# An attention and mixture-of-experts kernel on one Trainium2 core: the last routed block's products in another order, and the Silu of every block issued between its two halves

## Chip, core and metric

The kernel runs on one core of a Trainium2 chip. The metric is device time in microseconds, the median of several runs; smaller is better. The engines are TensorE (PE: matrix products; its weight loads are listed apart as PEld), VectorE (DVE), ScalarE (ACT), GpSimd (POOL) and SyncE (SP), which here only issues DMAs. Each engine carries out its own instructions in the order in which the program issues them, and waits on semaphores for the others.

## What is computed

The input is x of 8 x 256 rows, 512 long. A first layer adds a gated long convolution of the normalised x; it takes the first half of the time and isn't touched. The second layer, of the normalised result, is a mixture of experts of 2048 tokens:

```python
shared_out = silu(xf @ shared_wg.T) * (xf @ shared_wu.T) @ shared_wd.T      # inner width 704
h = silu(einsum('td,efd->etf', xf, exp_wg)) * einsum('td,efd->etf', xf, exp_wu)   # 8 experts, inner width 352
all_out = einsum('etf,edf->etd', h, exp_wd)
out = x + shared_out + sum over the 2 chosen experts of topk_w * all_out
```

All of it is float32. Only the two chosen experts of a token are computed.

## The kernel before

**Blocks.** The tokens are sorted by expert on the chip into blocks of up to 128 rows. 33 blocks are always worked through (`NSURE`): 25 with one expert each, 4 whose two halves of 64 rows have an expert each, and 4 in four groups of 32 rows, the last three groups of one expert. 20 more half-blocks stand inside an `If` (`rest_of_blocks`, L1875), which this input skips. The loop of L1887 takes the blocks in the order `seq`; the last one (`last`, index 32) is a block of one expert.

**One block.** A block's rows are gathered from `xn_d` by an indirect DMA of POOL, stored and reloaded by SP's DMAs in turned squares, and transposed by DVE (`block_T`). Then:

- `block_up` (L1776): the up products into a PSUM tile `up` of two halves, `ps[:, 0]` (gate) and `ps[:, 1]` (up). A half is 512 float32 wide, of which 352 are used, and fills one bank. For a block of one expert these are 4 products per half, issued half 0 first, then half 1; the trace lists each product as two passes. After all of them ACT takes the Silu of half 0 (L1790), and DVE multiplies it by half 1 (L1793; in the last block L1800, in an order that suits a transpose on PE).
- `block_hT` (L1818) transposes the result on DVE in 16 pieces. The last block uses `last_hT` (L1808) instead: three transposes on PE (L1813), copied from PSUM by ACT (L1814) and DVE (L1815).
- `block_down` (L1833): three down products (L1841, six passes) into a PSUM tile `y`, the scaling by the gate on ACT (`ys`, L1850), and an indirect DMA of POOL that adds the rows to `out` (L1854). These scatter-adds are ordered among themselves, since two of them can name the same row.

In the loop the down product of a block is issued two blocks later (L1908), so that its transposes are done; in the last three rounds it is the block before (L1910). The round of the last but two issues two down products.

**The end.** The shared expert's down products of the last two token tiles (`LATE`) are left for the end. `late_products` (L1916) issues them: for each tile five products of 512 columns (two passes each), and one of the short remainder (L1938). PE's order there is: up products of the last block, down product of the last but one, three transposes, one late product, down product of the last block, and the other late products. When the last scatter-add has landed, SP and ACT reload the two tiles' rows of `out` (L1934), DVE adds the late products (L1947), and SP and ACT store them (L1948).

**Order and waits.** The program is scheduled by hand (`manual_schedule`, L110): every engine gets its instructions in the order of the source. The waits between engines are made from the tiles that each instruction reads and writes. The shared expert's products (`seven`, L831) also use a two-bank PSUM tile, whose banks are written by PE and copied by ACT (L856) by turns; there, the program declares each product of one bank and each copy of the other to be independent:

```python
def free_of(ins, others):
    for other in others:
        tc.declare_no_dep(ins.ins, other.ins, reason="it is of the other bank")
```

`block_up` makes no such declaration.

Of the kernel before, what the change touches and what calls it, by code (L numbers as in the profile page):

```python
# [22 lines left out]
NLB = L // P  # L23
# [4 lines left out]
FF = 352  # L28
F_TILES = [(0, 128), (128, 128), (256, 96)]
SFF = 2 * FF  # L30
NSF = 6
# [47 lines left out]
def tile_xattn_moe(  # L79
# [29 lines left out]
    V, G, A, T, S = nc.vector, nc.gpsimd, nc.scalar, nc.tensor, nc.sync  # L109
# [993 lines left out]
    for c in range(NCHUNK):  # L1103
# [6 lines left out]
        if c == NCHUNK - 2:  # L1110
            at = len(steps) - TPC
# [319 lines left out]
    for h in range(H):  # L1431
# [15 lines left out]
        c, r = divmod(h - 10, 8)  # L1447
        nine, picks_here = h >= H9, c >= 0 and r == 2
        ready = done < h - 10 and steps[done][0] <= h
        between = copies = None  # L1450
        if c >= 0 and r == 7:
            make_down_sums(c, 0)
        if ready and is_begun(*steps[done][1:]):

            def between(at=steps[done][1:]):
                begun[at] = (begin_seven if at[0] is up_step else begin_down)(*at[1:])
                for _ in begun[at][0]():
                    pass
# [151 lines left out]
    wgu_sb = wgu_pool.tile([P, NEXP, NGU], F32, name="wgu_sb")  # L1610

    def load_wgu(e, n=2):
        m = 2 * NLB
        A.dma_start(
            out=wgu_sb[:, e : e + n].rearrange("p e (c f) -> p (e c) f", f=FF),
            in_=egu[e * m : (e + n) * m].rearrange("c p f -> p c f"),
        )
# [42 lines left out]
    xgs, xTs, eks = {}, {}, {}  # L1660
# [11 lines left out]
    def rows_in(b):  # L1672
        return P if b < NSURE else HP
# [27 lines left out]
    def load_ek(b):  # L1701

        i = b - NPURE
        e = nc.values_load(
            ek[0:1, b : b + 1] if i < 0 else eh[0:1, i : i + 1], engines=[PE], min_val=0,
            max_val=NEXP - 1 if i >= 0 else min(b, NEXP - 1),
            skip_runtime_bounds_check_because="an expert is a count of at most seven",
        )
        n = (P if i < 0 else Q if NPAIR <= i < NMIX else HP)
        eks[b] = [(slice(0, n), e)]  # L1710
        if 0 <= i < NMIX:
            eks[b] += [(slice(at, at + n), OWN[i]) for at in range(n, P, n)]

    def weights(sb, b, e, at, n):
        most = NEXP if b >= NPURE else min(b + 1, NEXP)
        w = sb[:, :most].rearrange("p e f -> p (e f)")
        at = e * sb.shape[2] + at
        return w[:, at : at + n] if isinstance(e, int) else w[:, bass.ds(at, n)]

    def block_T(b):  # L1720

        own = (rows, 3) if b < NSURE else (spare, 1)
        nq = rows_in(b) // Q
        xTs[b] = own[0].tile([P, NLB, NQ, Q], F32, tag="xT", name=f"xT_{b}", bufs=own[1])
        V.transpose(  # L1725
            xTs[b][:, :, :nq].rearrange("p k c b -> p c k b"),
            xgs.pop(b)[:, :nq].rearrange("p c (k a) -> p c k a", a=Q),
        )
# [4 lines left out]
    seq = list(range(NPURE))  # L1733
# [21 lines left out]
    def load_wd(e):  # L1755
        if e >= NEXP:
            return
        wde = wd_sb[:, e].rearrange("p (t d) -> p t d", d=L)
        S.dma_start(
            out=wde[:, 0:2, :], in_=ed[e, 0 : 2 * P].rearrange("(t p) d -> p t d", p=P)  # L1760
        )
        S.dma_start(out=wde[: FF - 2 * P, 2, :], in_=ed[e, 2 * P : FF])
# [10 lines left out]
    NF = len(F_TILES)  # L1773
    hs, hTb = {}, {}

    def block_up(k, last):  # L1776
        n = rows_in(k)
        ps = (ps_b if k < NSURE else ps_spare).tile([P, 2, L], F32, tag="up", name=f"up_{k}")
        for m in range(2):
            for j in range(NLB):  # L1780
                for at, e in eks[k]:
                    T.matmul(  # L1782
                        ps[at, m, :FF],
                        lhsT=xTs[k][:, j].rearrange("p c b -> p (c b)")[:, at],
                        rhs=weights(wgu_sb, k, e, (m * NLB + j) * FF, FF),
                        start=(j == 0),
                        stop=(j == NLB - 1),
                    )
        hk = (blk if k < NSURE else spare).tile([P, FF], F32, tag="h", name=f"h_{k}")
        A.activation(hk[:n], ps[:n, 0, :FF], AF.Silu)  # L1790
        xTs.pop(k)
        if not last:
            V.tensor_tensor(hk[:n], hk[:n], ps[:n, 1, :FF], ALU.mult)  # L1793
            hs[k] = hk
            return

        hp = blk.tile([P, NF, NQ, Q], F32, tag="h", name=f"hp_{k}")
        for q0, q1, n in ((0, NQ - 1, NF), (NQ - 1, NQ, NF - 1)):
            squares = slice(q0 * NF * Q, (q0 * NF + (q1 - q0) * n) * Q)
            V.tensor_tensor(  # L1800
                hp[:, :n, q0:q1].rearrange("p t q a -> p q t a"),
                hk[:, squares].rearrange("p (q t a) -> p q t a", t=n, a=Q),
                ps[:, 1, squares].rearrange("p (q t a) -> p q t a", t=n, a=Q),
                ALU.mult,
            )
        hs[k] = hp

    def last_hT(k):  # L1808
        hp = hs.pop(k).rearrange("p t q a -> p (t q a)")
        pt = ps_y.tile([P, NF, P], F32, tag="dn", name=f"hT_ps_{k}")  # L1810
        hT = blk.tile([P, NF, NQ, Q], F32, tag="hT", name=f"hTb_{k}")
        for ft, (f0, fw) in enumerate(F_TILES):
            T.transpose(pt[:fw, ft], hp[:, f0 : f0 + fw], ident)  # L1813
        A.copy(hT[:, : NF - 1].rearrange("p t c b -> p t (c b)"), pt[:, : NF - 1])  # L1814
        V.tensor_copy(hT[:fw, NF - 1].rearrange("p c b -> p (c b)"), pt[:fw, NF - 1])  # L1815
        hTb[k] = hT
# [16 lines left out]
    def block_down(k):  # L1833
        if k < NSURE:
            ps = ps_y.tile([P, L], F32, tag="dn", name=f"y_{k}")
        else:
            ps = ps_spare.tile([P, 2, L], F32, tag="up", name=f"y_{k}")[:, 0]
        hT = hTb.pop(k)
        for ft, (_, fw) in enumerate(F_TILES):
            for at, e in eks[k]:  # L1840
                T.matmul(  # L1841
                    ps[at],
                    lhsT=hT[:fw, ft].rearrange("p c b -> p (c b)")[:, at],
                    rhs=weights(wd_sb, k, e, ft * L, L)[:fw],
                    start=(ft == 0),
                    stop=(ft == NF - 1),
                )
        y = (blk if k < NSURE else spare).tile([P, L], F32, tag="y", name=f"ys_{k}", bufs=4 if k < NSURE else 1)
        n = rows_in(k)
        A.activation(y[:n], ps[:n], AF.Copy, scale=gate[:n, k : k + 1])  # L1850


        def send(at, index, col):
            G.indirect_dma_start(  # L1854
                out=out,
                out_offset=bass.IndirectOffsetOnAxis(
                    ap=index[: at.stop - at.start, col : col + 1], axis=0
                ),
                in_=y[at],
                in_offset=None,  # L1860
                bounds_check=NTOK + P - 1,
                oob_is_err=True,
                compute_op=ALU.add,
            )

        send(eks[k][0][0], row, k)
        if len(eks[k]) > 1:
            late.append((send, slice(eks[k][0][0].stop, P), second_row, k - NPURE))
# [17 lines left out]
    last = NSURE - 1  # L1886
    for k in range(NSURE):  # L1887
        if k + AHEAD < NSURE:
            load_ek(seq[k + AHEAD])
            if k > 0:  # L1890
                block_T(seq[k + AHEAD])
        if k > 0:
            load_wd(k + 1)
        if k in (2, 4):
            load_wgu(NEXP - 3 + k // 2, 1)
        if k + AHEAD + 3 < NSURE:
            gather(seq[k + AHEAD + 3])

        if k + AHEAD + 2 < NSURE:
            bring(seq[k + AHEAD + 2])  # L1900
        send_late()
        if k == REST_AT:
            rest_of_blocks()
        block_up(seq[k], k == last)
        if k < last:
            block_hT(seq[k])

        if 2 <= k < last - 1:  # L1908
            block_down(seq[k - 2])
        if k >= last - 2:  # L1910
            block_down(seq[k - 1])

    ps = ps_b.tile([P, LATE, L], F32, tag="up", name="dn_late")
    cols = [slice((TPC - LATE + i) * P, (TPC - LATE + i + 1) * P) for i in range(LATE)]

    def late_products(i, fts):  # L1916
        for ft in fts:
            T.matmul(
                ps[:, i],
                lhsT=hTs[last_c][:, ft, cols[i]],  # L1920
                rhs=wshd[:, ft, :],
                start=(ft == 0),
                stop=False,
            )

    last_hT(seq[last])
    late_products(0, range(1))
    block_down(seq[last])
    late_products(0, range(1, NSF - 1))
    late_rows = []  # L1930
    for i in range(LATE):
        t = NT - LATE + i
# [3 lines left out]
    for i in range(LATE):  # L1936
        at = slice(i * LAST, (i + 1) * LAST)
        T.matmul(  # L1938
            ps[:, i],
            lhsT=hTs[last_c][at, NSF - 1, cols[i]],  # L1940
            rhs=wshd[at, NSF - 1, :],
            start=False,
            stop=True,
# [98 lines left out]
```

## Time and profile before

| what | value |
|---|---|
| median of 3 runs | 738.3 us (738.06 to 738.66) |
| profiled execution, own time | 734.04 us |
| its span, first to last instruction | 732.2 us |
| mean granted TensorE clock | 0.999 |
| routed blocks, first up product to the last scatter's issue | 470.07 to 719.62 us |
| executed Silus of L1790 | 33 |
| DMA, mean over the span | 180 GB/s |

The profile is of a single execution, taken by the hardware profiler. A row of a timeline gives the start in us from the first instruction, the length, the engine, the source line and operation, the tiles (out<-in) and the number of merged instructions; in brackets stands how long the engine was idle before it and which instruction ended that. A row of the groups gives busy us and the mean ns of one instruction, then the idle us before the group and what ended it. The releaser is inferred from semaphores. Ends of matmuls are modelled, so successive passes overlap on paper; the time from start to start is what a pass costs in a stream.

### The profile page before, as it was taken

What the parts mean: (1) busy time and instruction counts of PE and PEld (TensorE: products, weight loads), DVE (VectorE), ACT (ScalarE), POOL (GpSimd) and SP (SyncE); (2) the same over time, 40 slices, a digit from 0 to 9 for tenths busy, and PEclk for the clock granted to TensorE, in tenths of its full rate; (3) what the DMA queues carried; (4) which work ended last, traced back from release to release, by engine and by line L of the source; (5) the groups of instructions that cost most, each with busy time, mean ns of one, the idle gap of its engine ahead of it and who ended that gap; (6) DMA issues with size and microseconds to landing.
All of it is one profiled execution on the core that took longest, in us unless ns stands there. A gap on an engine that the chain in (4) does not pass through costs nothing. (4 is left out here: it accounts for less than half of the span.)

```text
span 732.2 us, 10457 instructions
## 1 busy us (share of the span) xinstructions
PE 721.0 (98%) x3189; PEld 386.2 (53%) x3189; DVE 533.3 (73%) x1209; ACT 227.3 (31%) x459; POOL 405.4 (55%) x433
## 2 busy tenths in 40 slices
PE   9999999999999999999999999999999999999996
PEld 4333336555455655555665478455445444555552
DVE  4788889878677987777987574386786767758740
ACT  2222245745316554426435132011111111111110
POOL 7899898489776388794380422113344534424221
PEclk9999999999999999999999999999999999999999
DMA  8657748556635466525354968599876676666533
GB/s 284 226 186 276 282 141 267 181 121 193 205 106 193 136 163 195 178 86 170 112 130 139 378 180 276 178 278 313 242 170 127 124 157 149 128 156 146 88 43 86
DMA packets 91276, 131.62 MB, mean 180 GB/s; under 512 B 10896, under 2 KB 54928, under 8 KB 91216
## 3 DMA queue, kind: packets, MB, share of 16 engines
q1 hardware_dynamic: 69648, 93.37, 40.7%
q0 software_dynamic: 8544, 17.34, 13.2%
q10 hardware_dynamic: 13024, 20.19, 7.9%
q8 instruction: 28, 0.46, 0.2%
q14 instruction: 32, 0.26, 0.1%
HBM read 93.86 MB, written 37.00 MB: 179 GB/s over the span
## 5 line engine op out<-in xcount | busy, mean ns | idle before, releaser
L509 PE MATMUL cv<-kv,tz 64*64 64x512 f32 (+1 forms) x976 | 184.4, 597 | 0.3 <-DVE prod L585 0.3
L1782 PE MATMUL up<-wgu_sb,xT 128*128 (+5 forms) x784 | 162.4, 461 | 0.4 <-PEq L1876 0.4
L1825 DVE STREAM_TRANSPOSE hTb<-h 32x96 f32<-32x96 f32 (+1 forms) x512 | 133.8, 261 | 7.8
L460 POOL TENSOR_TENSOR kv<-vT,ctxT 128x512 f32<-128x512 f32 x127 | 131.6, 1069 | 11.9 <-DVE top L743 3.9
L1782 PEld LDWEIGHTS up<-wgu_sb,xT 128*128 128x128 f32 (+2 forms) x784 | 92.2, 155 | 75.3 <-issue 33.4
L509 PEld LDWEIGHTS cv<-kv,tz 64*64 64x64 f32 (+1 forms) x976 | 65.1, 145 | 109.5 <-issue 87.4
L1854 POOL DMA_INDIRECT out_dram<-ys,row x33 | 50.5, 1529 | 123.5 <-DMA out_dram<-ys,row 38.7
L1841 PE MATMUL y<-wd_sb,hTb 128*128 (+11 forms) x294 | 91.0, 595 | 0.0
L585 DVE TENSOR_TENSOR prod<-cv,ctxT 128x1024 f32<-128x1024 f32 x64 | 78.2, 1221 | 15.8 <-PE cv L509 14.1
L594 DVE TENSOR_REDUCE convT<-prod 128x128 f32<-128x1024 f32 x64 | 78.1, 1220 | 2.2
L844 PE MATMUL gu<-tb,wst 128*128 128x256 f32 x320 | 78.6, 381 | 0.6 <-ACT g L856 0.4
L1680 POOL DMA_INDIRECT picked<-xn_d,row x33 | 35.0, 1061 | 64.9 <-PE halves_ps L1317 19.5
L844 PEld LDWEIGHTS gu<-tb,wst 128*128 128x128 f32 x320 | 60.3, 190 | 17.3 <-issue 7.9
L1790 ACT ACTIVATE h<-up 128x352 f32<-128x352 f32 x33 | 15.3, 463 | 145.4 <-PE up L1782 145.4
L844 PE MATMUL gu<-xfT,wst 128*128 128x256 f32 x240 | 60.1, 386 | 0.2 <-DVE prod L585 0.2
L640 POOL TENSOR_TENSOR skip<-ctxT,w 128x512 f32<-128x512 f32 x16 | 17.2, 1075 | 74.6 <-DVE cv L582 38.7
L1841 PEld LDWEIGHTS y<-wd_sb,hTb 128*128 128x128 f32 (+5 forms) x294 | 34.3, 155 | 44.0 <-issue 38.7
L844 PEld LDWEIGHTS gu<-xfT,wst 128*128 128x128 f32 x240 | 44.2, 190 | 18.6 <-issue 12.1
L1850 ACT ACTIVATE ys<-y,gate 128x512 f32<-128x512 f32 x33 | 22.7, 687 | 73.1 <-PE y L1841 68.0
L509 PE MATMUL cv<-kv,td 128*128 128x512 f32 x88 | 45.2, 596 | 0.0
L801 POOL DMA_INDIRECT table<-entries,to x32 | 31.5, 985 | 19.2 <-DVE at L797 10.7
L1725 DVE STREAM_TRANSPOSE xT<-xg 128x512 f32<-128x512 f32 x33 | 23.5, 711 | 24.7 <-DMA xg<-picked_d 22.0
(266 smaller groups left out, 820.5 us busy)
## 6 DMA issues: line engine op xcount, KB each, us to landing
wst<-wst_d SPq DMA_DIRECT2D x17, 896.0 KB
tz<-in_toep_dram SPq DMA_DIRECT2D x32, 384.0 KB
wgu_sb<-in_egu_dram ACTq DMA_DIRECT2D x3, 2816.0 KB
picked_d<-picked SPq DMA_DIRECT2D x33, 256.0 KB
xg<-picked_d SPq DMA_DIRECT2D x132, 64.0 KB
ctxT<-in_cT_dram SPq DMA_DIRECT2D x16, 384.0 KB
x<-in_xv_dram SPq DMA_DIRECT2D x16, 256.0 KB
x<-in_x_dram SPq DMA_DIRECT2D x16, 256.0 KB
```

The lines of the kernel that those rows point to most:

```text
L460: engine.tensor_tensor(kvs[h][:, at], v[:, :, cols].unsqueeze(2).to_broadcast([P, B, NH, NH]), ctxT[t][:, at, :, cols].unsqueeze(3).to_bro ...
L509: return T.matmul(banks[lb][cols], lhsT=w, rhs=x, start=first, stop=all(left[lb][n] == 0 for n in here),)
L585: V.tensor_tensor(prod, ps.rearrange("p k b j i -> p (k b) j i"), ctxT[t][:, 2 + 2 * n : 4 + 2 * n, :, cols] .rearrange("p k b i -> p (k b ...
L594: V.tensor_reduce(convT[t][:, two, :, cols].rearrange("p k b j -> p (k b) j"), prod, AX.X, ALU.add)
L801: ins = G.indirect_dma_start(out=table, out_offset=bass.IndirectOffsetOnAxis(ap=to[:, i : i + 1], axis=0), in_=entry[:, i, n, :], in_offse ...
L844: ins = T.matmul(ps, lhsT=w[2 * a + k], rhs=x[:, k], start=start and k == 0, stop=k == 1, skip_group_check=True,)
L1680: G.indirect_dma_start(out=picked[:n], out_offset=None, in_=xn_d, in_offset=bass.IndirectOffsetOnAxis(ap=row[:n, b : b + 1], axis=0), boun ...
L1725: V.transpose(xTs[b][:, :, :nq].rearrange("p k c b -> p c k b"), xgs.pop(b)[:, :nq].rearrange("p c (k a) -> p c k a", a=Q),)
L1782: T.matmul(ps[at, m, :FF], lhsT=xTs[k][:, j].rearrange("p c b -> p (c b)")[:, at], rhs=weights(wgu_sb, k, e, (m * NLB + j) * FF, FF), star ...
L1825: V.transpose(hT[q * Q : (q + 1) * Q, :n, c], hk[c * Q : (c + 1) * Q, q * NF * Q : (q * NF + n) * Q].rearrange("p (t a) -> p t a", a=Q),)
L1841: T.matmul(ps[at], lhsT=hT[:fw, ft].rearrange("p c b -> p (c b)")[:, at], rhs=weights(wd_sb, k, e, ft * L, L)[:fw], start=(ft == 0), stop= ...
L1854: G.indirect_dma_start(out=out, out_offset=bass.IndirectOffsetOnAxis(ap=index[: at.stop - at.start, col : col + 1], axis=0), in_=y[at], in ...
```

## The change

`block_up`'s products move into a helper, `up_products`, that issues one half, or part of a half. The Silu of half 0 is now issued after half 0's products and before those of half 1, in every block. In the last block, after the first two of half 1's four products, `block_down` of the last but one is issued (its products, its scaling and its scatter-add), and then the other two. After the last block, one late product is issued ahead of `last_hT` and one behind it, where before there was one, behind. The number of products, transposes, activations and DMAs is the same.

```diff
+    def up_products(k, ps, m, js):
+        for j in js:
+            for at, e in eks[k]:
+                T.matmul(
+                    ps[at, m, :FF],
+                    lhsT=xTs[k][:, j].rearrange("p c b -> p (c b)")[:, at],
+                    rhs=weights(wgu_sb, k, e, (m * NLB + j) * FF, FF),
+                    start=(j == 0),
+                    stop=(j == NLB - 1),
+                )
+
-    def block_up(k, last):
+    def block_up(k, last, between=None):
...
-        for m in range(2):
-            for j in range(NLB):
-                for at, e in eks[k]:
-                    T.matmul(
...
+        up_products(k, ps, 0, range(NLB))
         hk = (blk if k < NSURE else spare).tile([P, FF], F32, tag="h", name=f"h_{k}")
         A.activation(hk[:n], ps[:n, 0, :FF], AF.Silu)
+        up_products(k, ps, 1, range(NLB // 2))
+        if between:
+            between()
+        up_products(k, ps, 1, range(NLB // 2, NLB))
...
-        block_up(seq[k], k == last)
+        block_up(seq[k], k == last, (lambda: block_down(seq[last - 1])) if k == last else None)
...
-        if k >= last - 2:
+        if last - 2 <= k < last:
             block_down(seq[k - 1])
...
+    late_products(0, range(1))
     last_hT(seq[last])
-    late_products(0, range(1))
+    late_products(0, range(1, 2))
     block_down(seq[last])
-    late_products(0, range(1, NSF - 1))
+    late_products(0, range(2, NSF - 1))
```

More of the change, by code (lines that the diff above doesn't have):

```diff
@@ L1774, in tile_xattn_moe @@
     hs, hTb = {}, {}
-    def block_up(k, last):
+    def up_products(k, ps, m, js):
[9 more added lines that the diff above has]
+    def block_up(k, last, between=None):
         n = rows_in(k)
         ps = (ps_b if k < NSURE else ps_spare).tile([P, 2, L], F32, tag="up", name=f"up_{k}")
-        for m in range(2):
-            for j in range(NLB):
-                for at, e in eks[k]:
[L1782 to L1788, printed above, removed]
+        up_products(k, ps, 0, range(NLB))
         hk = (blk if k < NSURE else spare).tile([P, FF], F32, tag="h", name=f"h_{k}")
         A.activation(hk[:n], ps[:n, 0, :FF], AF.Silu)
+        up_products(k, ps, 1, range(NLB // 2))
+        if between:
+            between()
+        up_products(k, ps, 1, range(NLB // 2, NLB))
         xTs.pop(k)
```

## The prediction

> **What bounds the kernel now.** I read the busy shares first, then the block stage by windows, then the tail by timeline, engine by engine. On the page's list of busy times and in its groups stand:
>
> ```profile
> PE 721.0 (98%) x3189; PEld 386.2 (53%) x3189; DVE 533.3 (73%) x1209; ACT 227.3 (31%) x459; POOL 405.4 (55%) x433
> ...
> L1790 ACT ACTIVATE h<-up 128x352 f32<-128x352 f32 x33 | 15.3, 463 | 145.4 <-PE up L1782 145.4
> ```
>
> TensorE is busy 98% of the span. A share is only an average, so next I take one ordinary block of the routed experts by itself; the columns are stretch, length, and then busy time (instructions) of each engine, granted clock, DMA share and GB/s:
>
> ```profile
> 501.58:508.89 7.31, 7.31 (x23) 4.18 (x22) 5.54 (x19) 1.15 (x2) 2.40 (x2) 1.00 1.09 334
> ```
>
> PE works through all of the 7.31 us. A block is 16 passes of the up products (each of the 8 products shows as two) and 6 passes of a down product: in the tail's rows below, up starts at 705.69 and down at 710.42, so a pass of 352 columns starts every 4.73/16 = 0.296 us, and the down's 6 passes take 713.00 - 710.42 = 2.58 us; 4.73 + 2.58 = 7.31. So there is no slack on PE: whatever idles PE inside a block is added to the time, once per block. DVE has 5.54 us of work per block and ACT 1.15, so neither is near it.
>
> The tail, PE then ACT, POOL, from timelines of the last 28 us:
>
> ```profile
> 705.69 4.90 PE L1782 MATMUL up<-wgu_sb,xT 128*128 x16
> 710.42 2.74 PE L1841 MATMUL y<-wd_sb,hTb 128*128 x6
> 713.00 0.49 PE L1813 MATMUL hT_ps<-ident,hp 128*128 128x128 f32 x3
> 713.33 1.02 PE L1918 MATMUL dn_late<-wshd,hT 128*128 128x512 f32 x2
> 714.25 2.84 PE L1841 MATMUL y<-wd_sb,hTb 128*128 x6
> ```
>
> ```profile
> 710.62 0.46 ACT L1790 ACTIVATE h<-up 128x352 f32<-128x352 f32 x1 [4.00 <-PE up L1782]
> 713.25 0.69 ACT L1850 ACTIVATE ys<-y,gate 128x512 f32<-128x512 f32 x1 [2.16 <-PE y L1841]
> 713.84 0.36 ACT L1814 COPY hTb<-hT_ps 128x256 f32<-128x256 f32 x1
> 717.18 0.69 ACT L1850 ACTIVATE ys<-y,gate 128x512 f32<-128x512 f32 x1 [2.98 <-issue]
> ```
>
> ```profile
> 708.25 1.55 POOL L1854 DMA_INDIRECT out_dram<-ys,row  x1 [4.13 <-issue]
> 714.21 1.55 POOL L1854 DMA_INDIRECT out_dram<-ys,row  x1 [4.42 <-ACT hTb L1814]
> 719.62 1.55 POOL L1854 DMA_INDIRECT out_dram<-ys,row  x1 [3.86 <-issue]
> ```
>
> The line that carries this prediction is the first of ACT's. The Silu reads half 0 (bank 0) of the up tile alone. Half 0 was full after 8 passes, near 705.69 + 8 x 0.296 + 0.16 = 708.2, and ACT sat idle. Yet the Silu starts at 710.62, 0.03 us after the end of **all** 16 passes (705.69 + 4.90 = 710.59), and the page's group shows the same wait on `PE up` before all 33. So in this program an access to one bank of the tile is ordered after matmuls into its other bank. The code says the same from the other side: where L856's copies and L844's products share a two-bank tile, each pair on different banks is declared independent by hand (L840); `block_up` declares nothing.
>
> The very end is a chain of scatter-adds into `out`: the last starts at 719.62, though its rows were ready at 717.18 + 0.69 = 717.87, because the one before must land first (5.41 us from start to start); it takes 4.75 us more by the chain view, and then come the reload, the add and the store.
>
> **The change part by part.**
>
> *Silu between the halves (all 33 executed blocks).* No instruction is added; the Silu is now issued before half 1's products. By the reading above it will wait for half 0 alone, but half 1's first product, issued behind a reader of the same tile, now waits for the Silu. Behind that product stand all later matmuls: PE has one queue. Its cost from rows, counted from the start of half 0's last pass: the pass lasts 0.46 us (median 459 ns for this line); the Silu starts 0.04 after it ends (0.03 to 0.07 over the blocks); it takes 0.46; PE restarts 0.05 after it, as here, where a product of L844 follows a copy of ACT:
>
> ```profile
> 434.19 0.37 ACT L856 COPY g<-gu 128x256 f32<-128x256 f32 x1
> ...
> 434.60 0.19 PEld L844 LDWEIGHTS gu<-tb,wst 128*128 128x128 f32 x1 [0.45 <-ACT g L856]
> ```
>
> and the first pass on a drained array is 0.10 longer (563 ns, this line's longest, against 459). Sum 0.46 + 0.04 + 0.46 + 0.05 + 0.10 = 1.11, less the 0.296 after which the next pass would have started anyway: **0.82 us per block**. Bounds: without the refill 0.72; with the slower restart of these rows (0.11 to the weight load, 0.15 to the matmul) 0.92:
>
> ```profile
> 112.04 0.38 ACT L856 COPY g<-gu 128x256 f32<-128x256 f32 x1
> ...
> 112.53 0.30 PEld L844 LDWEIGHTS gu<-tb,wst 128*128 128x128 f32 x2 [0.77 <-issue]
> 112.56 0.46 PE L844 MATMUL gu<-tb,wst 128*128 128x256 f32 x1 [0.40 <-ACT g L856]
> ```
>
> I take 0.82 because the wait is a single one, as at 434. In the four blocks of four groups the Silu starts 0.03 later; that adds 0.1 in all. ACT is free in time: the `ys` ahead of the last Silu runs from 705.94 to 706.63 and so ends 0.94 us after U = 705.69, half 0 needs 2.4.
>
> What the early Silu gives back: DVE's multiplication can start at the end of up instead of 0.5 us later. Worth nothing in the blocks, since the down product comes two blocks later.
>
> 32 blocks before the last: 32 x 0.82 + 0.1 = 26.3 us on the path. No DMA is issued earlier or later relative to its block; with PE slower the gathers and scatters only gain room.
>
> *The down product between the halves, last block.* U is the start of its up products (705.69 before). Half 0 ends its issue at U + 2.37, the stall makes it 3.19, two products of half 1 (4 passes) 4.37, the moved down 6.95, the rest of half 1 8.13. The `ys` of the moved down ends near U + 7.86 (before: 713.94 = U + 8.25), and its scatter starts 0.27 later, as at 714.21 before: U + 8.13 against 8.52. The scatter ahead of it started by U + 2.56, so with some 5.6 us it has landed (8.2 at worst, if nothing of that one moves). The gain here is 0.3 to 0.4.
>
> *Order of the late products.* DVE's `hp` runs from U + 8.34 to 8.93. Before, the down product covered it; now one late product (0.86 us of issue) does, to U + 8.99, so the transposes start there. The second late product covers ACT's and DVE's copies (to U + 10.2; before, DVE's ended at U + 8.83). If that cover were missing, PE would idle about 0.8. The last down then runs U + 10.19 to 12.93, its `ys` ends at 13.67, ready for the scatter at 13.94. By the scatter chain it could go at 8.13 + 5.41 = 13.54. So the last scatter starts at U + 13.94; before it was 719.62 = U + 13.93. The gain of the moved down product is eaten by the later last down: net 0.0, at most 0.4 either way. The remaining late products end near U + 20.9; the reloaded rows land near U + 21.9, so these stay hidden.
>
> *Sum.* 26.3 + 0.0 = 26.3 us on the profiled execution: 734.04 (span 732.2 and 1.84 around it) becomes 760.3. The median of the runs, 738.3, lies 4.26 above the profiled one; I carry that over unchanged: **764.6 us**.
>
> A rule speaks against this. The Trainium skill, "PSUM — Partial Sum Buffer", section "Summary: rules for kernel authors", says that PSUM may be read while a matmul runs if they are in different banks, and the Silu and half 1 are. By the rule no block would stall, and the time would be that of the first rival, 737.9. The row at 710.62 is about which waits this program has, not about what the banks allow, so I go by the row.
>
> **The rivals.**
>
> *No wait between the banks* (ends not slower). The waits on `up` could hold one way only, or the Silu's late start come from how PE's completions are counted, and half 1 run beside the Silu. For it: half 1 touches no byte that the Silu reads. Against: 33 of 33 Silus waited for the whole tile. Then U is unmoved, the moved down ends 0.82 earlier, its scatter goes at 8.25 + 5.6 = 713.85 or so, held by the one of 708.25, the last one 5.41 later at 719.26 (its own rows are ready at U + 13.12 = 718.81): 0.36 us gained, **737.9**. It cannot gain more, as the scatters' chain holds it. The deciding point is whether half 1's first pass starts 0.3 or 1.1 us after half 0's last.
>
> *The clock falls too.* With a pause in each block the granted clock could drop. Against: a window of 186 to 194 us, in which PE was busy for only 6.64 of 8 us, has the clock at 1.00. If it fell by a tenth, the stage's some 250 us would grow by about 25 more: **790**.
>
> **How the numbers follow.** Stall in all blocks 0.92, no wait 0.05, clock or another dear effect 0.03. With 0.72 to 0.92 per block and 0.4 either way at the end: 738.3 + 32 x 0.72 - 0.4 = 760.9, and 738.3 + 32 x 0.92 + 0.1 + 0.4 = 768.2. I give 760.5 to 769; what is left out is 0.05 below and 0.03 above and a little of the likeliest case. 0.2% (1.5 us) is about what a measurement of this kernel can tell from no change: slower 0.95 (the stall and the clock), the same 0.04 and faster 0.01 (both from the case without a wait, whose 0.36 us is inside that bound).
>
> **What would show it.** Right: waits of PE on `ACT h` 33 times, some 0.55 us each as PE's idle time; an ordinary block of 8.1 us instead of 7.31, PE busy about 95% of the span; Silus 2.4 us earlier in their block; the last scatter within 0.4 us of U + 13.9. Wrong: blocks still 7.31 us long with no idle PE (first rival), PEclk below 1.00 in the block stage (second), or PE waits at L1813 and L1841 in the tail of more than 0.3 us.

## The result, and the profile after

The changed kernel takes 768.93 us (median of 6 runs, 767.67 to 772.92); the kernel before, run beside it, 739.98 (738.06 to 742.63). The ratio is 1.0394, 95% interval 1.0359 to 1.0429. The forecast was 764.6, a ratio of 1.0356: the sign and the cause hold, the size was about a tenth too small. The profiled execution took 768.45 us, its span 766.4.

The first lines of the changed kernel's page, and its groups of the up products and the Silu:

```profile
PE 732.2 (96%) x3189; PEld 383.0 (50%) x3189; DVE 534.3 (70%) x1209; ACT 227.6 (30%) x459; POOL 405.7 (53%) x433
...
L1779 PE MATMUL up<-wgu_sb,xT 128*128 (+5 forms) x784 | 172.1, 467 | 22.4 <-ACT h L1792 20.8
...
L1792 ACT ACTIVATE h<-up 128x352 f32<-128x352 f32 x33 | 15.3, 464 | 77.2 <-PE up L1779 50.5
```

The same 3189 matmuls, but the up products now stand idle for 22.4 us (0.4 before), of which the Silu ended 20.8. In the Silu's view it is named as the releaser 32 times; the 33rd pause, 0.70 us at 624.30 in one of the mixed blocks, is there too, put down to "issue":

```profile
who waited for it (us, times):
  PEld up L1779: 39.3, 32
  PE up L1779: 20.8, 32
```

An ordinary block by windows, and the last two blocks on PE by timeline:

```profile
696.32:704.45 8.13, 7.58 (x23) 4.09 (x22) 5.41 (x19) 1.15 (x2) 2.66 (x2) 1.00 0.55 127
```

```profile
734.51 2.63 PE L1779 MATMUL up<-wgu_sb,xT 128*128 x8 [0.55 <-ACT h L1792]
736.99 2.74 PE L1847 MATMUL y<-wd_sb,hTb 128*128 x6
739.56 2.53 PE L1779 MATMUL up<-wgu_sb,xT 128*128 x8
742.65 1.45 PE L1779 MATMUL up<-wgu_sb,xT 128*128 x4 [0.55 <-ACT h L1792]
743.94 2.74 PE L1847 MATMUL y<-wd_sb,hTb 128*128 x6
746.51 1.35 PE L1779 MATMUL up<-wgu_sb,xT 128*128 x4
```

The block is 8.13 us long instead of 7.31. The 16 passes have split in two: half 0 from 739.56 to 742.09, a pause of 0.55, half 1 from 742.65. The pause plus the refill (2.63 against 2.53 for eight passes) plus the overlap that is lost make 0.82.

One block is different. In block 4 (the fifth) of the changed kernel, PE and ACT by timeline, and the block by windows:

```profile
500.31 2.53 PE L1779 MATMUL up<-wgu_sb,xT 128*128 x8
506.29 3.76 PE L1779 MATMUL up<-wgu_sb,xT 128*128 x8 [3.46 <-ACT h L1792]
509.84 3.36 PE L1847 MATMUL y<-wd_sb,hTb 128*128 x6
```

```profile
505.28 0.40 ACTq L1614 DMA_DIRECT2D wgu_sb<-in_egu_dram  x1
505.78 0.46 ACT L1792 ACTIVATE h<-up 128x352 f32<-128x352 f32 x1 [4.58 <-DVE hTb L1831]
```

```profile
500.31:513.04 12.73, 9.27 (x24) 4.90 (x23) 8.23 (x29) 1.15 (x2) 2.66 (x2) 0.87 1.07 310
```

Half 0 is ready at 502.84. The Silu starts at 505.78, because ACT's queue holds the issue of an expert's weight load (`load_wgu`, L1614) ahead of it, which could not go before 505.28. By the trace's semaphores the load waited for a transfer that SP had issued at 499.06 (`xg<-picked_d`), which landed at 505.26. After 3.46 us of idleness PE's passes are slower for a while (3.76 us for eight, 3.36 for six of 512 columns that take 2.74), and the granted clock of the stretch is 0.87. So this block is 5.42 us longer than before, 0.82 + 4.60; of the 4.60, 2.91 is the longer pause (3.46 against 0.55) and 1.7 the slower passes. In the profile before, the same issue stood at 498.33, 4.06 us into its block, and delayed nothing, since the Silu then started after 4.93 us:

```profile
498.33 0.40 ACTq L1614 DMA_DIRECT2D wgu_sb<-in_egu_dram  x1
499.20 0.46 ACT L1790 ACTIVATE h<-up 128x352 f32<-128x352 f32 x1 [4.05 <-PE up L1782]
```

The Trainium skill, "TensorE: Matmul & The Clock Gate", section "What's actually happening", has the array's clock halved after one idle window of about 3.4 us. The pause of 3.46 us agrees with it, and so does one of 3.59 us in the first stage of the run "Declared independent" below. Shorter pauses in the first stages of "Two tiles" and "The load behind the Silu" don't follow one bound: the clock fell after 2.20 us and stayed after 2.80. The three pauses in this order, and the 5 us behind each, with the granted clock as the third figure from the end:

```profile
168.76 1.13 PE L844 MATMUL gu<-tb,wst 128*128 128x256 f32 x4 [3.59 <-ACT g L856]
308.06 1.14 PE L844 MATMUL dn<-wT,xfT 128*128 128x256 f32 x4 [2.20 <-ACT dg L856]
193.26 1.10 PE L844 MATMUL dn<-wT,xfT 128*128 128x256 f32 x4 [2.80 <-ACT dg L856]
...
168.76:173.76 5.00, 5.00 (x15) 4.14 (x16) 3.59 (x4) 1.74 (x5) 3.15 (x4) 0.66 0.39 118
308.06:313.06 5.00, 5.00 (x16) 4.10 (x17) 4.06 (x4) 1.64 (x5) 3.25 (x4) 0.66 0.61 178
193.26:198.26 5.00, 5.00 (x22) 4.06 (x22) 4.06 (x4) 2.02 (x6) 3.24 (x4) 1.00 0.54 156
```

So the runs show that the pause of block 4 was long enough, and not that 3.4 us is the least that lowers the clock.

Where the profiled executions differ: 768.45 - 734.04 = 34.4 us, of which 34.2 lie in the spans (766.4 - 732.2); the rows below add up to that but for rounding.

| stretch | us |
|---|---|
| up to the first block (470.07 and 472.74) | 2.7 |
| 32 steps of the blocks, 0.78 to 0.91 each | 26.2 |
| block 4 beyond that | 4.6 |
| the step across the `If` beyond that | 0.4 |
| last block and the end (26.52 and 26.88) | 0.4 |

The first row is not the change's. PE's order up to the first block is the same in all kernels here, and in the other eight profiles that follow the blocks begin between 473.4 and 479.7, in kernels that are as fast as before too. The profile before was a short one, as its own time (734.04) beside the median shows.

### The profile page after: what moved, and what is told of

Same layout as the page of the kernel before. It is cut to its first block, busy times and chain, and to the rows that moved or that the text cites. A ratio compares the mean times of both kernels' runs of the same rounds, so it can differ in the third digit from the quotient of the medians.

```text
span 766.4 us, 10473 instructions
## 1 busy us (share of the span) xinstructions
PE 732.2 (96%) x3189; PEld 383.0 (50%) x3189; DVE 534.3 (70%) x1209; ACT 227.6 (30%) x459; POOL 405.7 (53%) x433
## 5 line engine op out<-in xcount | busy, mean ns | idle before, releaser
L1779 PE MATMUL up<-wgu_sb,xT 128*128 (+5 forms) x784 | 172.1, 467 | 22.4 <-ACT h L1792 20.8
L1779 PEld LDWEIGHTS up<-wgu_sb,xT 128*128 128x128 f32 (+2 forms) x784 | 89.7, 155 | 109.0 <-ACT h L1792 39.3
L1799 DVE TENSOR_TENSOR h<-h,up 128x352 f32<-128x352 f32 x32 | 16.6, 517 | 81.7 <-PE up L1779 81.7
```

The costliest lines, as they stand in the source:

```text
L1779: T.matmul(ps[at, m, :FF], lhsT=xTs[k][:, j].rearrange("p c b -> p (c b)")[:, at], rhs=weights(wgu_sb, k, e, (m * NLB + j) * FF, FF), star ...
```

## Experiments

The theory after the result: half 1's first product waits for the Silu through a wait that the program makes, 0.82 us in each block; block 4 is the order on ACT's queue; the tail is worth nothing. The rivals: the hardware or the place on ACT costs the time, not the wait; the tail holds a part of the loss; block 4 was a hiccup.

**Two tiles.** The change's order, each half in a PSUM tile of its own:

```diff
-        ps = (ps_b if k < NSURE else ps_spare).tile([P, 2, L], F32, tag="up", name=f"up_{k}")
+        own = ps_b if k < NSURE else ps_spare
+        ps = [own.tile([P, L], F32, tag=f"up{m}", name=f"up{m}_{k}") for m in range(2)]
```

> Edit: the order of the change is kept, but each half of up gets a PSUM tile of its own, one bank each (the two late sums too). Theory (half 1's first product waits for the Silu because both touch one tile, though not one bank): no wait of PE on ACT h is left, an ordinary block takes 7.31 us again and not 8.13, block 4 loses its 5.4 us too, as PE no longer asks for the Silu there; ratio to before 0.999 to 1.001. Rival (reading one bank while products fill the next costs time on the chip itself, or the Silu's new place on ACT's queue does): blocks of 8.1 us remain, ratio near 1.035.

Measured: 741.47 us, ratio 1.0014 (0.9985 to 1.0042). The whole list of PE's waits from the first block to the end, and block 4 on PE and ACT:

```profile
PE up L1779 <- PEq L1883: 0.6, 1, 0.6
```

```profile
501.79 4.90 PE L1779 MATMUL up<-wgu_sb,xT 128*128 x16
506.52 2.74 PE L1848 MATMUL y<-wd_sb,hTb 128*128 x6
```

```profile
507.38 0.40 ACTq L1614 DMA_DIRECT2D wgu_sb<-in_egu_dram  x1
507.88 0.46 ACT L1793 ACTIVATE h<-up 128x352 f32<-128x352 f32 x1 [5.21 <-DMA wd_sb<-in_ed_dram]
```

All 33 pauses are gone, and counted from the first block every block starts where the kernel before has it, to 0.01 us up to the `If` and 0.1 us later behind it. In an ordinary block the Silu starts 2.57 us in, beside half 1's products. In block 4 the load is issued late again and the Silu starts at 507.88, 6.1 us into the block; PE doesn't ask for it and loses nothing. So neither the early Silu nor a late one costs anything by itself: the wait does.

**Declared independent.** The two-bank tile stays, but the products of half 1 are declared as those of L840 are:

```diff
+                if silu:
+                    tc.declare_no_dep(ins.ins, silu.ins, reason="it is of the other bank")
```

> Edit: the change with its two-bank tile kept, but each product of half 1 is declared independent of the Silu, as the shared expert's products are. Theory (the stall is a wait that the program makes, not something that the banks or ACT impose): no wait of PE on ACT h, ordinary blocks 7.31 us, ratio 0.997 to 1.003, the same as with two tiles. Rival (the split into two tiles brought the time back by another way, such as other bank addresses): blocks stay near 8.13 us, ratio near 1.035.

Measured: 739.56 us, ratio 1.0004 (0.9978 to 1.0030); no wait of PE on the Silu, and each block as long as before to 0.01 us. The whole list of PE's waits from the first block to the end:

```profile
PE up L1779 <- PEq L1884: 0.4, 1, 0.4
```

The same tile and the same order without the wait give the time back, so it was no matter of bank addresses. It also bears on the rule that was weighed in the prediction (the Trainium skill, "PSUM — Partial Sum Buffer", section "Summary: rules for kernel authors": read a bank other than the one that a matmul is writing). The case agrees: with the Silu reading one bank beside products that fill the next, no block became longer. What the row of the Silu showed, and what cost the time, is that this program orders whole tiles unless it is told otherwise.

**A second reader.** The Silu is issued twice between the halves:

```diff
         A.activation(hk[:n], ps[:n, 0, :FF], AF.Silu)
+        A.activation(hk[:n], ps[:n, 0, :FF], AF.Silu)
```

> Edit: the change with the Silu issued twice in a row between the halves (same input, same output), so that half 1 has two readers to wait for. Theory (PE's pause is the drain, the reader's time and the restart): PE's pause grows by the second activation, 0.46 us, and up to 0.2 for its wait on the first one's write; the step per block goes from 0.82 to 1.28 to 1.5 us; another 15 to 22 us on the change, ratio 1.058 to 1.072. Rival (PE waits for something else of fixed length, the drain of the array or a semaphore's way): step stays near 0.82, ratio near 1.04.

Measured: 782.27 us, ratio 1.0598 (1.0567 to 1.0628). PE and ACT by timeline:

```profile
574.15 2.63 PE L1779 MATMUL up<-wgu_sb,xT 128*128 x8
577.84 2.34 PE L1779 MATMUL up<-wgu_sb,xT 128*128 x7 [1.05 <-ACT h L1793]
```

```profile
576.82 0.46 ACT L1792 ACTIVATE h<-up 128x352 f32<-128x352 f32 x1 [1.87 <-issue]
577.32 0.46 ACT L1793 ACTIVATE h<-up 128x352 f32<-128x352 f32 x1
```

PE's pause goes from 0.55 to 1.05, the step per ordinary block from 0.82 to 1.32: 0.46 of the second activation and 0.04 between the two. The pause is the reader's time plus a fixed way there and back, as the terms of the prediction have it.

**The early Silu in the last block only.** What is left of the change is its tail:

```diff
+        if last:
+            A.activation(hk[:n], ps[:n, 0, :FF], AF.Silu)
         up_products(k, ps, 1, range(NLB // 2))
...
         up_products(k, ps, 1, range(NLB // 2, NLB))
+        if not last:
+            A.activation(hk[:n], ps[:n, 0, :FF], AF.Silu)
```

> Edit: the Silu goes back behind all up products in every block but the last; the moved down product and the late products stay as changed. Theory (the tail's part is worth about nothing, and all of the loss is the Silu's in 32 blocks): one wait of PE on ACT h, 0.55 us idle, in the last block; last scatter 13.9 to 14.1 us after the last block's start; ratio 0.999 to 1.001. Rival (the tail's new order costs what the forecast missed, some 8 us on the profiled runs): ratio 1.005 to 1.011.

Measured: 739.77 us, ratio 1.0016 (0.9979 to 1.0054); one wait on the Silu, in the last block. The loss is the Silu's, not the tail's. One number missed: the last scatter starts 724.28 - 709.50 = 14.78 us after the last block's start, not 13.9 to 14.1. The scatters of the last four blocks on POOL:

```profile
707.54 1.55 POOL L1863 DMA_INDIRECT out_dram<-ys,row  x1 [4.05 <-DMA out_dram<-ys,row]
713.05 1.55 POOL L1863 DMA_INDIRECT out_dram<-ys,row  x1 [3.97 <-ACT h L1793]
718.55 1.55 POOL L1863 DMA_INDIRECT out_dram<-ys,row  x1 [3.95 <-DMA out_dram<-ys,row]
724.28 1.55 POOL L1863 DMA_INDIRECT out_dram<-ys,row  x1 [4.18 <-ACT ys L1859]
```

They follow each other at 5.5 to 5.7 us, and the last goes later than its own rows allow (its `ys` ends at 723.31; 0.27 later would be U + 14.08): here the chain was already late when the last block began (its third last started at U + 3.55, in the profile before at U + 2.56), so bringing the rows earlier gains nothing, and the end came 27.49 us after U, 1.0 later than before. With the stall in every block, as in the change, the chain keeps up. That the chain decides was in the prediction; how late it would be in this kernel was not seen.

**The early Silu without the tail.** In all blocks, with the end as before:

```diff
-        block_up(seq[k], k == last, (lambda: block_down(seq[last - 1])) if k == last else None)
+        block_up(seq[k], k == last)
...
-    late_products(0, range(1))
     last_hT(seq[last])
-    late_products(0, range(1, 2))
+    late_products(0, range(1))
```

> Edit: the Silu stays between the halves in all blocks, but the tail is as before (down product of the last but one behind the whole up, one late product behind the transposes). Theory: 0.82 us for each of 33 blocks, 4.6 more in block 4, and now the last block's stall is not made up for by the moved down product: the last scatter starts near 14.7 us after the last block's start; ratio 1.040 to 1.044, 0 to 1 us slower than the change as a whole. Rival (a part of the loss is the tail's): clearly faster than the change, ratio 1.03 or less.

Measured: 767.98 us, ratio 1.0397 (1.0362 to 1.0433). It has the loss of the whole change. The ratio lies just below the expectation; block 4 cost only 0.9 us beyond its 0.82 in this profile, not 4.6. The last scatter starts 14.87 us after the last block's start (14.7 expected, 14.08 in the change): the tail's edit does win 0.8 us here, which is the last block's own stall.

**The load behind the Silu.** The change, with ACT's two weight loads after `block_up`:

```diff
-        if k in (2, 4):
-            load_wgu(NEXP - 3 + k // 2, 1)
...
         block_up(seq[k], k == last, (lambda: block_down(seq[last - 1])) if k == last else None)
+        if k in (2, 4):
+            load_wgu(NEXP - 3 + k // 2, 1)
```

> Edit: the change, with the two loads of expert weights that ACT issues in blocks 2 and 4 put behind the block's Silu instead of ahead of it. Theory (in block 4 ACT stands at the load's issue until 5 us into the block; the Silu queues behind it, PE behind the Silu, and PE's clock falls after the long pause): the step of block 4 falls from 5.42 us to 0.82, clock 1.00 there, total 4.6 us less than the change: ratio 1.032 to 1.036. Rival (the pause there is a hiccup of DMA or clock that has nothing to do with the order on ACT): block 4 still 4 to 6 us longer, ratio 1.038 to 1.042.

Measured: 767.41 us, ratio 1.0390 (1.0358 to 1.0423), which is above the expectation and within that of the rival. Block 4 by itself is as expected, PE and ACT by timeline:

```profile
505.75 2.63 PE L1779 MATMUL up<-wgu_sb,xT 128*128 x8 [0.55 <-ACT h L1792]
508.22 2.74 PE L1847 MATMUL y<-wd_sb,hTb 128*128 x6
```

```profile
505.23 0.46 ACT L1792 ACTIVATE h<-up 128x352 f32<-128x352 f32 x1 [1.68 <-PE up L1779]
508.33 0.40 ACTq L1614 DMA_DIRECT2D wgu_sb<-in_egu_dram  x1
```

The load is issued behind the Silu, the pause is the ordinary 0.55, the step 0.82. Here too the load went late, 5.66 us into the block, so that a Silu behind it would have been late. The place on the queue is shown as the cause of block 4's loss; its size in an average run is not, since the times of a few runs can't tell 0.7 from 4.6 us.

**The change once more.**

> The changed kernel once more, nothing edited. Ordinary blocks 0.82 us longer than before, as in the first profile. Open: block 4. If its 5.4 us belong to the order of ACT's instructions, the step there is again above 0.82, but its size goes by when the load can be issued (0.9 to 5); if the first profile caught a hiccup, it is 0.82. Ratio 1.036 to 1.043.

Measured: 771.50 us, ratio 1.0446 (1.0419 to 1.0472), a little over the expectation. Its profiled execution, the fastest of them, took 767.28 us: ordinary blocks 0.82, block 4 1.53, the first block 1.27 (0.91 in the first profile). The median lies 4.2 us above this execution, and no trace shows where. ACT in block 4, which starts at 503.18:

```profile
503.38 0.69 ACT L1856 ACTIVATE ys<-y,gate 128x512 f32<-128x512 f32 x1 [5.30 <-PE y L1847]
505.93 0.43 ACTq L1614 DMA_DIRECT2D wgu_sb<-in_egu_dram  x1
506.46 0.46 ACT L1792 ACTIVATE h<-up 128x352 f32<-128x352 f32 x1 [2.39 <-DMA xg<-picked_d]
```

Four profiles have the load ahead of an early Silu with the wait. Block 4 was late in three of them (4.60, 0.92 and 0.71 us beyond the rest), but not in that of the second reader, which begins the block at 503.98:

```profile
505.56 0.44 ACTq L1614 DMA_DIRECT2D wgu_sb<-in_egu_dram  x1
506.55 0.46 ACT L1792 ACTIVATE h<-up 128x352 f32<-128x352 f32 x1 [1.68 <-PE up L1779]
```

There the load went 1.57 us into the block, before half 0 was full at 2.53, and held nothing up; in the three it went 4.97, 2.96 and 2.75 us into it. So it is no hiccup, but its size goes by when the load can be issued, from nothing to 4.6 us in four profiles.

**An earlier catch-up.** Two tiles, the round with two down products one block earlier, the second late product behind the last down product:

```diff
-        if 2 <= k < last - 1:
+        if 2 <= k < last - 2:
             block_down(seq[k - 2])
-        if last - 2 <= k < last:
+        if last - 3 <= k < last:
             block_down(seq[k - 1])
...
-    late_products(0, range(1, 2))
     block_down(seq[last])
-    late_products(0, range(2, NSF - 1))
+    late_products(0, range(1, NSF - 1))
```

> Edit: two tiles for up as in the first run, the round with two down products comes one block earlier, so that the scatter-adds catch up before the end, and the second late product goes back behind the last down product. Theory of the tail (the last scatter's start is set by the later of its own rows and the scatter before it): scatters of the last three blocks start near 1.2, 7.3 and 12.9 us after the last block's start (before: 2.6, 8.5, 13.9); from there to the end 25.4 to 25.7 us instead of 26.5; 0.8 to 1.1 us gained, ratio 0.996 to 1.002, which the times alone can hardly show. Rival (the tail is bound by the late products on PE or by the reload): the end does not move, 26.1 us or more after the last block's start.

Measured: 738.66 us, ratio 0.9996 (0.9975 to 1.0016): no difference that the times show. By the profile the last three scatters start 1.7, 7.3 and 13.2 us after the last block's start, and the end comes after 25.99 us instead of 26.52. So the end comes 0.5 us earlier than before, half of what was expected, and even that isn't shown to be the earlier round's: with the same end as the change, "Two tiles" ended after 26.10 us and "Declared independent" after 26.47. The scatter of the last but two was still held by the one before it, 5.6 us earlier, and the last one waited for its own rows, whose `ys` begins at U + 12.22 and takes 0.69, as the last down product began at 9.29.

## What was right in the prediction, and which step failed

**The wait.** Right, as to cause and size. The step of an ordinary block was forecast at 0.82 and measured at 0.82 in every profile with the order of the change and the wait; PE's pause, forecast at 0.55, measured 0.55. The restart took the short way of the row at 434, not that of 112. In the four blocks of four groups it is 0.79, 0.79, 0.79 and 0.91 instead of 0.85, together 3.28 = 4 x 0.82; the added 0.1 us was not there. 32 steps make 26.2 us against 26.3.

**"ACT is free in time."** This step failed. It looked at the activation in front of the last block's Silu alone, not at the DMA issues on ACT's queue in the other blocks, and so put the wait for ACT at nothing: in block 4 the Silu was moved, as seen from PE, to a time at which ACT can still stand at a weight load. (The load of block 2 goes while block 1 still runs, at 481.06 in the first profile, and delays nothing.) Before, the row at 498.33, 0.9 us ahead of the Silu of 499.20, showed it. In the two profiles of the changed kernel it costs 4.6 and 0.7 us, all in block 4, the larger with PE's clock falling. The stated bounds have no room for it: of the ten executions of the changed kernel in the two sets six took more than 769 us, and their median is 769.4. "PEclk below 1.00 in the block stage" was named as the mark of the second rival; it did occur, in one block, behind this wait and not behind the regular 0.55 us pauses, during which the clock stayed at 1.00.

**What else was missed.** The step across the `If` at block 24 is 0.3 to 0.9 us longer in all five profiles with the stall and 0.0 to 0.1 in the four other variants. The prediction had no term for it. PE's queue is named as the releaser; why the stall makes the step longer was not tried and stays open.

**The tail.** Right: the moved down product's scatter was forecast at U + 8.13 and started at 747.73 - 739.56 = 8.17; the last one at 13.94, and started at 14.08. Net 0.0 forecast, 0.4 us measured.

**The base.** The profile before began its blocks at 470.07, earlier than any other; carrying its 4.26 us to the median over unchanged was right in kind, but the medians of before lie between 738.3 and 740.0 from one set of runs to the next, so that 1.7 of the 4.3 us between 764.6 and 768.93 is this (739.98 beside the change, 738.3 in the prediction). The rest is what the change itself costs more, 28.95 us instead of 26.3. With 27.3 us (32 steps, `If` and tail as in the profile with the load behind) and 0.7 to 4.6 for block 4, the change comes to 28 to 32 us, 1.038 to 1.043 of 740; measured were 1.0394 and 1.0446, the second a little above it.

**The rivals.** "No wait between the banks" is refuted for this program. Its price, a gain of 0.4 us, fits what came where the wait was taken away (two tiles, or declared): PE lost nothing, and the times show no gain (1.0014 and 1.0004), but they can't tell 0.4 us from none.

## What to carry to other kernels

Ask of each reader that is moved up between two groups of products what the next product will now wait for: where waits are made per tile, a bank of its own doesn't make it independent, and the price is the drain, the reader, the restart and the refill, once per repetition, on an engine that was 98% busy. An instruction that another engine waits for takes with it everything that stands ahead of it on its own queue, DMA issues too (up to 4.6 us in block 4). Give each half its own tile, or declare the independence, before the order is changed; and look at whether the end is bound by the thing that is made earlier (here it was a chain of scatter-adds).

## What the runs showed of the hardware

After a pause of 3.46 us PE ran eight passes of 352 columns in 3.76 us instead of 2.63, and the granted clock of the block was 0.87; 0.55 us in every 8.13 left it at 1.00, and 1.05 us in every 8.63 too (mean granted clock of that execution 0.998). Which length of pause lowers the clock stays open: 2.20 us was once followed by 0.66 over 5 us, 2.80 us once by 1.00. The first stage of the same program varied by up to 9.6 us between profiles, with the stall or without (blocks beginning at 470.07 to 479.65), more than the tail's edits are worth; why is open, and only a comparison block by block shows what the edits did.
